# A third nested product in an attention output projection, with ScalarE reading the plain products and GpSimd adding them

## The chip, the cores and the metric

The kernel runs on one core of a Trainium2 chip. TensorE (PE) does the matrix products, VectorE (DVE), ScalarE (ACT) and GpSimd (POOL) work around it, SyncE (SP) issues most of the transfers, and each takes its instructions in a written order. Results of TensorE land in PSUM; operands and results of the others lie in SBUF. The metric is the device time of one execution in microseconds (us), lower being better; the median of three executions is quoted.

## The reference, cut to what matters

The input `x` is 8 images of 512 channels by 1024 positions, all in float32. Each image goes through self-attention with a residual, and then through a non-local block whose last step is a normalisation over the whole batch:

```python
q = conv1x1(x, Wq, bq); k = conv1x1(x, Wk, bk); v = conv1x1(x, Wv, bv)   # 8 heads of 64 channels
attn = softmax(einsum('bhdn,bhdm->bhnm', q, k) * scale)
out = einsum('bhnm,bhdm->bhdn', attn, v).reshape(B, C, H, W)
x = x + conv1x1(out, Wp, bp)                       # "p": the output projection
g, theta, phi = conv1x1 of x, each to 256 channels # "tp": theta and phi together
f = einsum('bcn,bdn->bcd', theta, phi) / n
z = conv1x1(einsum('bcd,bdn->bcn', f, g), W_w, W_b) + x
z_hat = (z - mean over batch and positions) * rsqrt(var + eps) * gamma + beta
```

The change is in `p`, a product of a 512 x 512 weight with a 512 x 1024 matrix for each image, which is added into `x`.

## The kernel before, in words

Images are worked on one after the other in the loop over `b` (L1063 to L1209). Within an iteration TensorE goes through the attention of image `b`, the projections q, v and k of image `b + 1`, then `p` of image `b`, then `tp`, `g` and the rest of the non-local block of image `b`. All these projections use Strassen's scheme in Winograd's form: a matrix product is split into 2 x 2 blocks and done with seven block products instead of eight, with sums and differences of blocks formed beforehand. `SEVEN` (L286) lists them: which weight block, which data block, which PSUM slot, and which quarters of the result the slot is read into. Products that share a slot accumulate in it, so the slot is read once after each of them and the later reads hold the running sum.

A block product can itself be done by seven smaller products: it is then called nested. One plain product of `p` is four matmuls of 128 x 512; a nested one is seven matmuls of 128 x 256. In the profile each float32 matmul appears as two records. `nested` (L305) issues the small matmuls one step at a time, and the list of counts in `INNER` (L302) says how many steps follow each plain matmul. For `p` of the images 1 to 6 the list `FIVE` (L297) has five plain products, and two products are nested, (1, "21", "11") and (2, "t4", "21"). The images 0 and 7 use seven plain ones.

`seven` (L333) takes the four PSUM slots in the order of the list `free`: the plain products use the first two, the nested ones the last two. Each slot holds 128 x 1024 numbers. After a product with nested partners, `free` is rotated by one, so that the first slot of the next product (`tp`) is the second plain slot of `p`. A slot that is taken by the next product waits until everything that reads it has ended.

`project` (L775) is `p`: VectorE reads each plain product out of PSUM and adds it to the quarters of `x` it belongs to, with the bias where the quarter is first touched (L782), else without (L477). The nested products are read in the same way, 128 x 256 at a time. The result then serves `tp` as data, together with four differences of quarters, `t1` to `t4` (`more_sums`, L262).

What `p` reads is prepared by GpSimd during k of the next image: the normalised attention output `o` (L729), the sums of the nested blocks (`inner_sums`, L279), four differences of quarters of `o` (L267), and then k's own four last additions (L402, at the end of `six`, L383), in this order.

Weights are kept in device memory in units of one to three blocks and loaded again for each image (`fetch`, L160). `UNITS` (L117) says which blocks form a unit; a unit with two blocks has room for the inner sums of both, and units are loaded through a ring of four buffers. Instructions recorded with `pe`, `dve` or `sp` (one function, L62) keep the program's order on their engine; each engine does its own in order, and a waiting instruction holds those behind it.

Of the kernel before, what the change touches and what calls it, by code (L numbers as in the profile page):

```python
# [8 lines left out]
F32 = mybir.dt.float32  # L9
# [7 lines left out]
P = 128  # L17
# [13 lines left out]
def unshifted(ctx: ExitStack, tc: tile.TileContext, a: dict, out: bass.AP):  # L31
# [79 lines left out]
    for b in range(1, B):  # L111
# [2 lines left out]
    loaded, ahead = [], {"unit": [], "first": []}  # L114

    PAIRS = ((1, 6), (3, 4), (5, 2))
    UNITS = {"WqT": PAIRS, "WkT": PAIRS, "WvT": PAIRS, "WpT": ((1, 2), (3, 4, 5), (6,)), "tp": ((1, 2), (3, 4, 5), (6,)),  # L117
             "WgT": (range(7),)}
    WIDTH = 14 * P

# [39 lines left out]
    def fetch(w, n, t=None, dma=None):  # L160
        dma, name = dma or nc.sync, w.name
        if t is None:
            t = wf0.tile([P, 2 * w.half], F32, tag="w0", name=f"w0_{name}") if n == "first" else \
                wr.tile([P, WIDTH], F32, tag="w", name=f"w_{name}_{n}")
        blocks = w.place(n, t)
        if name in kept:
            of = kept["plain" if w.last else name][n]
            sp(dma.dma_start(w.whole(n) if w.last else w.tiles[n], of))
            return
        if n == 0:  # L170
            corner[name] = block(f"a21_{name}")[:, :, :w.half]
# [36 lines left out]
    def inner_weights(w, i):  # L208

        a11, a12, a22, a21, s2, s3, s4 = w.inner(i)  # L210
        return [lambda to=to, l=l, r=r, op=op: dve(nc.vector.tensor_tensor(to, l, r, op))
                for to, l, r, op in ((s3, a11, a21, ALU.subtract), (a21, a21, a22, ALU.add), (s2, a21, a11, ALU.subtract),
                                     (s4, a12, s2, ALU.subtract))]

    def nest(w, i):
        for one in inner_weights(w, i):
            one()
# [64 lines left out]
    def quarters_of(t):  # L282
# [16 lines left out]

    INNER = {"p": (FIVE, ((1, "21", "11", False), (2, "t4", "21", True)), [0] * 4 + [1] * 14),  # L302
             "tp": (FIVE, ((2, "t4", "21", True), (1, "21", "11", False)), [0] * 24 + [1] * 14)}

    def nested(name, w, data, tags, first, add, goes_to, positions_out):  # L305
# [25 lines left out]
                yield  # L331

    def seven(name, w, data, positions_out, first, add, between=None, early=False,  # L333
              by_chunk=False, inner=None):

        nk, half = w.shape[2], w.shape[3]
        tags = list(free)
        free[:] = [tags[3], tags[1], tags[0], tags[2]] if early else [tags[3], tags[1], tags[2], tags[0]]  # L340
        slots, begun = {}, set()
        steps, counts = iter(()), iter(())
        if inner:
            free[:] = [tags[1], tags[2], tags[3], tags[0]]
            products, goes_to, counts = INNER[inner]
            counts = iter(counts)
            steps = nested(name, w, data, tags[2:], first, add, goes_to, positions_out)
        else:
            products = LATER if early == "later" else EARLY if early else SEVEN

        def read(reads, ps):
            for to, is_first in reads:
                (first if is_first else add)(to, ps)

        for n, (what, wi, di, s, reads) in enumerate(products):
            if s not in slots or early and what == "t4":
                slots[s] = bank(tags[s], f"{name}_{s}_{n}")
                begun -= {one for one in begun if one[0] == s}
            ps, d = slots[s], data[di]
            if positions_out:  # L360
                parts = [(ps.rearrange("p h (i f) -> p (h i) f", f=half)[:, i, :], i * half // 512,
                          lambda k, i=i: d[:, k, i * P:(i + 1) * P], lambda k: w[:, wi, k, :])
                         for i in range(512 // P)]
            else:
                parts = [(ps[:, m, :], m, lambda k, m=m: w[:, wi, k, m * P:(m + 1) * P], lambda k: d[:, k, :])
                         for m in range(half // P)]
            work = [(*part, k) for part in parts for k in range(nk)]
            if by_chunk and what in ("11", "s1t1"):
                work.sort(key=lambda one: one[4])
            for i, (to_ps, at, lhsT, rhs, k) in enumerate(work):  # L370
                pe(nc.tensor.matmul(to_ps, lhsT(k), rhs(k), start=(s, at) not in begun, stop=(k == nk - 1),  # L371
                                    skip_group_check=True))
                begun.add((s, at))
                for _ in range(next(counts, 0)):
                    next(steps)
            read(reads, ps)
            if between and n in between:
                between[n]()

    SIX = (((1, "21", "11"), (6, "22", "12")), ((3, "t1", "22"), (4, "t2", "T6")), ((5, "t3", "T7"), (2, "t4", "21")))  # L380
    ORDER = "0a 0b 1a 2a 2b 1b 5a 4a 5b 4b 3a 3b 6a 6b".split()

    def six(name, w, data, positions_out, at, begin, third, fills, by_scalar=False):  # L383

        fills = dict(fills)
        shape = [P, 4, 256] if positions_out else [P, 2, 512]
# [75 lines left out]
        assert not fills, fills  # L462
        if by_scalar:
            add("T7", "T6")
        add("22", "T7")
        add("21", "T7")

    def rows(q):
        return q[0] if isinstance(q[0], slice) else slice((int(q[0]) - 1) * CC // 2, int(q[0]) * CC // 2)
# [65 lines left out]
    def heads_of(b, what, w, bias, data, pin=lambda ins: None, steps=None, fills=None, **how):  # L535

        t = mats.tile([P, CC, N], F32, tag=what, name=f"{what}_{b}")

        if fills is not None:
            def begin(to, ps, i):  # L540
                nc.scalar.activation(to, ps, AF.Identity, bias=bias[:, i:i + 1])

            def third(to, ps, of, i):
                if what == "q":
                    nc.scalar.activation(to, ps, AF.Identity, bias=steps[:, i:i + 1])
                else:
                    dve(nc.vector.scalar_tensor_tensor(to, ps, steps[:, i:i + 1], of, ALU.add, ALU.add))

            six(f"p{what}_{b}", w, data, False, lambda q: t[:, rows(q), cols(q)], begin, third, fills,
                what == "q")  # L550
# [12 lines left out]
        return t  # L563
# [211 lines left out]
    def project(b, xt, w, between, data):  # L775
# [12 lines left out]

# [274 lines left out]
    for b in range(B):  # L1063
        last = b == B - 1
        nxt = {}
        if b == 1:
            nest(w_tp, 1)
            nest(w_tp, 2)
            keep("tp", w_tp, (0,))
            load_w()  # L1070
# [39 lines left out]
        if not last:  # L1110
# [20 lines left out]
            k = heads_of(b + 1, "k", weights("WkT"), bk, data, dve, steps=dk, fills={  # L1131
                (0, 13): [*o_sums, *(more if b else ())], (1, 13): () if b else more,
                (2, 0): () if b else [lambda: dve(nc.vector.tensor_tensor(bp, bp, got, ALU.add)),
                                      lambda: weight_sums(w_p, corner["WpT"], (6,), dve, nc.gpsimd)]})
# [302 lines left out]
```

## Time and profile before

| | |
|---|---|
| median of three executions | 2103.23 us (2102.15 to 2103.65) |
| the profiled execution's own time | 2103.74 us |
| its span, from the first to the last instruction | 2102.0 us |
| TensorE busy | 2078.5 us, 99% of the span |
| VectorE busy | 1442.3 us, 69% |
| ScalarE busy | 788.6 us, 38% |
| GpSimd busy | 734.0 us, 35% |
| mean clock granted to TensorE | 0.996 of full speed |
| DMA queue of SP | 31.8% of the 16 engines' span |

A row of the groups of instructions reads: line, engine, operation, output and inputs by the program's names, shapes and count, then the busy time, the mean duration of one in ns, and the idle time just before them with what ended it. A row of the timeline reads: start, length, engine, line, operation, operands, count of merged instructions, and in brackets an idle time and what ended it. All times are us from the span's start unless marked ns. Matmuls are pipelined, so the spacing of their starts says more than their durations.

### The profile page before, as it was taken

Reading aid. Unit: us, or ns where it says so; the run is one execution under the profiler, and the core shown is the slowest. Engines: PE = TensorE matmul, PEld = TensorE weight load, DVE = VectorE, ACT = ScalarE, POOL = GpSimd, SP = SyncE. Lnnn points to the kernel's source line nnn. Section 1 sums busy time; section 2 is a strip of 40 time slices with the busy share of each in tenths; the row PEclk is TensorE's granted clock in tenths of the full one; section 3 lists DMA queues with packets and bytes.
Section 4 is the critical chain, followed back from the end, with each engine's and each line's share of the span. In section 5 each row is a group of like instructions: output and inputs, shape, how many; then the busy total and the mean of one; then the engine's idle time right before and its main releaser. Section 6 shows DMA issues by size and latency. Waiting matters only on the chain.

```text
span 2102.0 us, 34269 instructions
## 1 busy us (share of the span) xinstructions
PE 2078.5 (99%) x13646; PEld 1170.3 (56%) x13646; DVE 1442.3 (69%) x2169; ACT 788.6 (38%) x1043; POOL 734.0 (35%) x637
## 2 busy tenths in 40 slices
PE   9999999999999999999999999999999999999995
PEld 4535864358733677336773377633776348743472
DVE  5587567875677656776567766677665775676756
ACT  1465203652046410464105641066312653056106
POOL 0024800348113581134812356123660338411010
PEclk9999999999999999999999999999999999999998
DMA  6254534345343443435324363253644345212668
GB/s 230 83 144 78 162 137 143 42 83 157 105 115 38 89 148 106 119 39 114 132 92 122 40 142 122 69 126 40 155 149 154 39 48 174 99 30 40 218 253 321
DMA packets 77263, 246.80 MB, mean 117 GB/s; under 512 B 17188, under 2 KB 25640, under 8 KB 75048
## 3 DMA queue, kind: packets, MB, share of 16 engines
q1 hardware_dynamic: 63224, 218.17, 31.8%
q0 software_dynamic: 12016, 24.80, 12.2%
q8 instruction: 110, 1.80, 0.4%
q10 hardware_dynamic: 1856, 1.56, 0.3%
q14 instruction: 57, 0.47, 0.1%
HBM read 163.20 MB, written 47.71 MB: 100 GB/s over the span
## 4 chain that ended last, share of the span: by engine, by line
PE 98%; ACT 1%; DVE 1%; DMA 0%; issue 0%; DVEq 0%
PE ps L611 21%; PE po L637 21%; PE pp L371 7%; PE ptp L371 7%; PE pv_in L447 6%; PE pq_in L450 6%; PE pk_in L450 6%; PE pg L371 5%; PE pz L371 3%; PE pf L866 2%; PE ptp_in_s L319 2%; PE pp_in_s L322 2%; PE pwf L909 1%; PE pv L414 1%; PE pq L417 1%; PE pq L371 1%
## 5 line engine op out<-in xcount | busy, mean ns | idle before, releaser
L614 ACT ACTIVATE e<-ps 128x1024 f32<-128x1024 f32 x512 | 522.4, 1024 | 428.7 <-PE ps L611 418.0
L667 POOL DMA_DIRECT2D fold<-acc x336 | 257.2, 816 | 949.2 <-DMA fold<-acc 450.4
L620 DVE TENSOR_TENSOR acc<-acc,e 128x1024 f32<-128x1024 f32 x384 | 469.9, 1224 | 94.5 <-ACT e L614 84.6
L611 PE MATMUL ps<-q,k 64*64 64x512 f32 x4096 | 529.3, 589 | 0.0
L637 PE MATMUL po<-e,v 64*64 64x512 f32 x4096 | 528.8, 589 | 0.0
L637 PEld LDWEIGHTS po<-e,v 64*64 64x64 f32 x4096 | 156.7, 133 | 282.8 <-issue 275.5
L611 PEld LDWEIGHTS ps<-q,k 64*64 64x64 f32 x4096 | 155.6, 133 | 283.1 <-issue 274.9
L897 ACT ACTIVATE g<-pg,gb 128x512 f32<-128x512 f32 x31 | 21.3, 687 | 447.7 <-PE pg L371 447.6
L618 DVE TENSOR_TENSOR acc<-e,e 128x1024 f32<-128x1024 f32 x64 | 78.3, 1224 | 117.6 <-ACT e L614 115.4
L371 PE MATMUL pp<-t_o,w_WpT 128*128 128x512 f32 x208 | 101.0, 592 | 0.0
L371 PE MATMUL ptp<-w_tp,t_x 128*128 128x256 f32 x400 | 96.1, 379 | 0.0
L729 POOL TENSOR_TENSOR o<-o,r 128x1024 f32<-128x1024 f32 x28 | 65.5, 2359 | 36.0 <-DMA r<-den_d 35.5
L371 PEld LDWEIGHTS ptp<-w_tp,t_x 128*128 128x128 f32 x400 | 72.3, 190 | 7.8
L458 DVE TENSOR_TENSOR k<-k,pk_in 128x256 f32<-128x256 f32 x112 | 46.8, 421 | 39.4 <-PE pk_in L450 35.0
L371 PE MATMUL ptp<-w_tp,x 128*128 128x256 f32 x272 | 69.6, 380 | 0.0
L371 PE MATMUL pp<-o,w_WpT 128*128 128x512 f32 x144 | 67.7, 592 | 0.0
L456 ACT COPY v<-pv_in 128x256 f32<-128x256 f32 x84 | 31.4, 374 | 95.8 <-DVE T_pv L458 25.5
L458 DVE TENSOR_TENSOR v<-v,pv_in 128x256 f32<-128x256 f32 x112 | 46.2, 421 | 29.3 <-PE pv_in L447 22.8
L456 ACT COPY k<-pk_in 128x256 f32<-128x256 f32 x84 | 31.2, 372 | 93.3 <-PE pk_in L450 91.6
L782 DVE SCALAR_TENSOR_TENSOR x<-pp,bp,x 128x512 f32<-128x512 f32 x52 | 37.5, 746 | 33.0 <-PE pp L371 33.0
L447 PE MATMUL pv_in<-w_WvT,i_t_x 128*128 128x128 f32 x448 | 59.2, 275 | 0.0
L450 PE MATMUL pk_in<-i_t_x,w_WkT 128*128 128x256 f32 x224 | 58.1, 381 | 0.1
(246 smaller groups left out, 3166.0 us busy)
## 6 DMA issues: line engine op xcount, KB each, us to landing
fold<-acc POOLq DMA_DIRECT2D x336, 64.0 KB, 3.0
w_WqT<-kept_WqT SPq DMA_DIRECT2D x21, 896.0 KB, 5.9
w_WvT<-kept_WvT SPq DMA_DIRECT2D x21, 896.0 KB, 5.5
w_WkT<-kept_WkT SPq DMA_DIRECT2D x21, 896.0 KB, 6.7
r<-den_d SPq DMA_DIRECT2D x32, 512.0 KB, 7.7
x<-in_x_dram SPq DMA_DIRECT2D x30, 512.0 KB, 6.0
spill<-x SPq DMA_DIRECT2D x24, 512.0 KB, 4.3
z<-spill SPq DMA_DIRECT2D x24, 512.0 KB, 8.1
```

What stands on the lines that cost most here:

```text
L371: pe(nc.tensor.matmul(to_ps, lhsT(k), rhs(k), start=(s, at) not in begun, stop=(k == nk - 1), skip_group_check=True))
L447: pe(nc.tensor.matmul(ps[:, i, :], d[:, i * P:(i + 1) * P], a, start=start and not i, stop=True, skip_group_check=True))
L450: pe(nc.tensor.matmul(ps, a, d, start=start, stop=True, skip_group_check=True))
L456: nc.scalar.copy(piece(q, i, j), ps)
L458: dve(nc.vector.tensor_tensor(piece(q, i, j), piece(q, i, j), ps, ALU.add))
L611: pe(nc.tensor.matmul(ps[c * P // 2:(c + 1) * P // 2, j, :], k[r, p, keys], q[r, p, h * 512:(h + 1) * 512], start=True, stop=True, skip_gr ...
L614: nc.scalar.activation(e, ps, AF.Exp, scale=SCALE)
L618: nc.vector.tensor_tensor(accs[u], es[u, 0], e, ALU.add)
L620: ins = nc.vector.tensor_tensor(accs[u], accs[u], e, ALU.add)
L637: pe(nc.tensor.matmul(ps[j * D:(j + 1) * D, r, :], v[keys, m, (2 * p + j) * D:(2 * p + j + 1) * D], e[keys, j, :], start=(m == 0), stop=(m ...
L667: nc.gpsimd.dma_start(to, of, accum_op=ALU.add)
L729: dve((engine or nc.vector).tensor_tensor(at, at, of, ALU.mult))
```

## The change

For the images 1 to 6, `p` gets a third nested product: `FIVE` gives way to `FOUR`, with four plain products, and the nested ones are now (6, "22", "12"), (2, "t4", "21") and (1, "21", "11"), in this order. The third nested product uses the same PSUM columns as the first. The last plain product, `s3t3`, takes a new tile in the second plain slot instead of accumulating in the first.

The plain products `s1t1` and `s2t2` are no longer read by VectorE. ScalarE copies each into a block in SBUF (two copies of 128 x 512), and GpSimd adds that block into the quarters it belongs to, two for `s1t1` and three for `s2t2` (128 x 1024 each). The last two additions of k on GpSimd are moved behind them (`later`). The difference `t1` of `tp`'s data moves ahead of the reads of the last plain product, and `t2` stands directly behind them.

Block 6 needs inner sums: for the units of WpT to have room, they become (1, 2), (3, 4), (5, 6). The inner sums of block 6 are made once, at the start of image 1, in a tile of their own (`nest_apart`), and stored; from then on block 5 and the widened block 6 are loaded with two transfers. For image 0 the sums of the weight blocks 5 and 6 go to VectorE, and the addition of the small bias goes from VectorE to GpSimd.

```diff
-    UNITS = {"WqT": PAIRS, "WkT": PAIRS, "WvT": PAIRS, "WpT": ((1, 2), (3, 4, 5), (6,)), "tp": ((1, 2), (3, 4, 5), (6,)),
+    UNITS = {"WqT": PAIRS, "WkT": PAIRS, "WvT": PAIRS, "WpT": ((1, 2), (3, 4), (5, 6)), "tp": ((1, 2), (3, 4, 5), (6,)),
...
-            sp(dma.dma_start(w.whole(n) if w.last else w.tiles[n], of))
+            if n == 2 and name == "WpT" and not w.last:
+                sp(dma.dma_start(w[5], of[:, 0, :].rearrange("p (k f) -> p k f", k=2)))
+                sp(dma.dma_start(w.tiles[n][:, WIDTH // 2:], kept["block 6"]))
+            else:
+                sp(dma.dma_start(w.whole(n) if len(of.shape) == 3 else w.tiles[n], of))
...
+    def nest_apart(w, n, i):
+
+        t = w3.tile([P, N], F32, tag="acc", name="apart")[:, :WIDTH // 2]
+        to = t[:, :2 * w.half]
+        sp(nc.sync.dma_start(to, kept["plain"][n][:, 1, :]))
+        w.at[i] = to.rearrange("p (k f) -> p k f", k=2)
+        w.extra[i] = t[:, 2 * w.half:].rearrange("p (i f) -> p i f", i=3)
+        nest(w, i)
+        kept[f"block {i}"] = dram.tile([P, WIDTH // 2], F32, tag=f"block{i}", name=f"block{i}")
+        sp(nc.sync.dma_start(kept[f"block {i}"], t))
...
-    INNER = {"p": (FIVE, ((1, "21", "11", False), (2, "t4", "21", True)), [0] * 4 + [1] * 14),
+    FOUR = (SEVEN[0], ("s1t1", 3, "t1", 1, (("22", False), ("12", False))),
+            ("s2t2", 4, "t2", 0, (("12", False), ("22", False), ("21", False))),
+            ("s3t3", 5, "t3", 1, (("22", True), ("21", False))))
+
+    INNER = {"p": (FOUR, ((6, "22", "12", True), (2, "t4", "21", True), (1, "21", "11", False)),
+                   [1] * 10 + [2, 1] + [2] * 4),
...
-            if s not in slots or early and what == "t4":
+            if s not in slots or early and what == "t4" or inner == "p" and what == "s3t3":
...
-            read(reads, ps)
+            if inner and ahead_of_last and n == len(products) - 1:
+                ahead_of_last()
+            if inner and what in via:
+                via[what](reads, ps)
+            else:
+                read(reads, ps)
...
-        add("22", "T7")
-        add("21", "T7")
+        ends = [lambda q=q: add(q, "T7") for q in ("22", "21")]
+        if later is not None:
+            later += ends
+            return
+        for one in ends:
+            one()
...
-                if b == B - 1 and q in ("11", "22"):
+                if b == B - 1 and q in ("11", "22") or b and ps.shape[-1] == 512 and q == "22":
                     dve(ins)
 
+        def by_scalar(reads, ps):
+            t = block(f"read_{b}")
+            for m in range(2):
+                nc.scalar.copy(t[:, m, :], ps[:, m, :])
+            for q, _ in reads:
+                at = xt[:, rows(q), cols(q)]
+                dve(nc.gpsimd.tensor_tensor(at, at, t, ALU.add))
+            if len(reads) == 3:
+                for one in later:
+                    one()
+
         seven(f"pp_{b}", w, data, False, first, add_to(xt), between, early=b == B - 1 and "later",
-              inner="p" if 0 < b < B - 1 else None)
+              inner="p" if 0 < b < B - 1 else None,
+              via={"s1t1": by_scalar, "s2t2": by_scalar}, ahead_of_last=lambda: more_sums(x1, (1,), dve))
...
         if b == 1:
+            nest_apart(Weights("WpT"), 2, 6)
             nest(w_tp, 1)
...
-                o_sums = [lambda: inner_sums(nxt["o"], "21", dve, nc.gpsimd), *o_sums]
+                o_sums = [*(lambda of=of: inner_sums(nxt["o"], of, dve, nc.gpsimd) for of in ("22", "21")), *o_sums]
...
-                more = [lambda i=i: weight_sums(w_p, corner["WpT"], (i,), dve, nc.gpsimd) for i in (3, 4, 5)]
+                more = [lambda i=i: weight_sums(w_p, corner["WpT"], (i,), dve, nc.gpsimd) for i in (3, 4)]
...
-                (2, 0): () if b else [lambda: dve(nc.vector.tensor_tensor(bp, bp, got, ALU.add)),
-                                      lambda: weight_sums(w_p, corner["WpT"], (6,), dve, nc.gpsimd)]})
+                (2, 0): () if b else [lambda: dve(nc.gpsimd.tensor_tensor(bp, bp, got, ALU.add))]})
+            if b == 0:
+                weight_sums(w_p, corner["WpT"], (5, 6), dve)
...
-        project(b, xt, w, between, nxt["o"])
+        x1 = data_sums(quarters_of(xt), f"x1_{b}", ())
+        project(b, xt, w, between, nxt["o"], x1, later if 0 < b < B - 1 else ())
...
-        data = data_sums(quarters_of(xt), f"x1_{b}", (1, 2, 3, 4) if last else (1, 2))
+        data = x1
+        if 0 < b < B - 1:
+            more_sums(data, (2,), dve)
+        else:
+            more_sums(data, (1, 2, 3, 4) if last else (1, 2))
```

More of the change, by code (lines that the diff above doesn't have):

```diff
@@ L333, in seven @@
     def seven(name, w, data, positions_out, first, add, between=None, early=False,
-              by_chunk=False, inner=None):
+              by_chunk=False, inner=None, via=(), ahead_of_last=None):
         nk, half = w.shape[2], w.shape[3]
@@ L381, in unshifted, with six @@
     ORDER = "0a 0b 1a 2a 2b 1b 5a 4a 5b 4b 3a 3b 6a 6b".split()
-    def six(name, w, data, positions_out, at, begin, third, fills, by_scalar=False):
+    def six(name, w, data, positions_out, at, begin, third, fills, by_scalar=False, later=None):
         fills = dict(fills)
@@ L549, in heads_of @@
             six(f"p{what}_{b}", w, data, False, lambda q: t[:, rows(q), cols(q)], begin, third, fills,
-                what == "q")
+                what == "q", how.get("later"))
             return t
@@ L773, in attention, with project @@
         return o["o"], all_denominators, normalize
-    def project(b, xt, w, between, data):
+    def project(b, xt, w, between, data, x1, later=()):
         def first(q, ps):
@@ L1126, in unshifted @@
                 more = [lambda: inner_sums(nxt["o"], "t4", dve, nc.gpsimd)]
-                o_sums = [lambda: inner_sums(nxt["o"], "21", dve, nc.gpsimd), *o_sums]
+                o_sums = [*(lambda of=of: inner_sums(nxt["o"], of, dve, nc.gpsimd) for of in ("22", "21")), *o_sums]
             else:
                 w_p = loaded[1]
-                more = [lambda i=i: weight_sums(w_p, corner["WpT"], (i,), dve, nc.gpsimd) for i in (3, 4, 5)]
-            k = heads_of(b + 1, "k", weights("WkT"), bk, data, dve, steps=dk, fills={
+                more = [lambda i=i: weight_sums(w_p, corner["WpT"], (i,), dve, nc.gpsimd) for i in (3, 4)]
+            later = [] if b else None
+            k = heads_of(b + 1, "k", weights("WkT"), bk, data, dve, steps=dk, later=later, fills={
                 (0, 13): [*o_sums, *(more if b else ())], (1, 13): () if b else more,
-                (2, 0): () if b else [lambda: dve(nc.vector.tensor_tensor(bp, bp, got, ALU.add)),
-                                      lambda: weight_sums(w_p, corner["WpT"], (6,), dve, nc.gpsimd)]})
+                (2, 0): () if b else [lambda: dve(nc.gpsimd.tensor_tensor(bp, bp, got, ALU.add))]})
+            if b == 0:
+                weight_sums(w_p, corner["WpT"], (5, 6), dve)
         else:
```

## The prediction

> **What bounds the kernel now.** I first read the page's busy shares and chain, then TensorE's waits.
>
> ```profile
> PE 2078.5 (99%) x13646; PEld 1170.3 (56%) x13646; DVE 1442.3 (69%) x2169; ACT 788.6 (38%) x1043; POOL 734.0 (35%) x637
> ...
> PE 98%; ACT 1%; DVE 1%; DMA 0%; issue 0%; DVEq 0%
> ```
>
> ```profile
> PE count L1223 <- DVE good L1221: 8.6, 1, 8.6
> PE warm_ps L500 <- DVE zeros L483: 1.1, 1, 1.1
> PE pk_in L450 <- DVE T_pk L547: 1.1, 1, 1.1
> ```
>
> TensorE is the path, and it waits three times in all. So matmul time removed is time saved, and any new wait of TensorE is lost one for one: nothing on the path can absorb it. Next I read the timeline around `p` of image 1, for TensorE and then GpSimd and VectorE.
>
> ```profile
> 514.38 3.60 PE L371 MATMUL pp<-o,w_WpT 128*128 128x512 f32 x8
> 517.82 1.02 PE L371 MATMUL pp<-t_o,w_WpT 128*128 128x512 f32 x2
> 518.67 0.59 PE L322 MATMUL pp_in_s<-o,w_WpT 128*128 128x256 f32 x2
> 519.11 1.02 PE L371 MATMUL pp<-t_o,w_WpT 128*128 128x512 f32 x2
> ...
> 537.59 3.62 PE L371 MATMUL ptp<-w_tp,x 128*128 128x256 f32 x16
> ```
>
> ```profile
> 502.28 0.73 POOL L279 TENSOR_TENSOR i_o<-o 128x256 f32<-128x256 f32 x1
> ...
> 517.51 2.36 POOL L402 TENSOR_TENSOR k<-k 128x1024 f32<-128x1024 f32 x1
> 519.95 6.96 POOL L402 TENSOR_TENSOR k<-k,T_pk 128x1024 f32<-128x1024 f32 x3
> 541.42 2.35 POOL L267 TENSOR_TENSOR t_x<-x,t_x 128x1024 f32<-128x1024 f32 x1 [14.51 <-DVE t_x L267]
> ```
>
> ```profile
> 533.07 1.22 DVE L477 TENSOR_TENSOR x<-x,pp 128x1024 f32<-128x1024 f32 x1 [0.44 <-PE pp L371]
> ...
> 537.79 2.35 DVE L477 TENSOR_TENSOR x<-x,pp 128x1024 f32<-128x1024 f32 x2 [1.23 <-PE pp L371]
> 540.06 1.22 DVE L267 TENSOR_TENSOR t_x<-x,t_x 128x1024 f32<-128x1024 f32 x1
> ```
>
> Four plain matmuls take 517.82 - 514.38 = 3.44 us, so 0.86 each; a plain and a nested one take 519.11 - 517.82 = 1.29, so a nested one takes 0.43. `p` lasts 537.59 - 514.38 = 23.21 us, which is 20 x 0.86 + 14 x 0.43: no gap. GpSimd is busy without a break until 526.9, well into `p`. VectorE's reads of the last plain product (537.79 to 540.1) run while TensorE is already in `tp`. That works because `tp`'s first slot is the second plain slot of `p`, whose last read (533.07) had ended at 534.29.
>
> **What the Trainium skill says.** "Perfetto Trace Analysis", under Tensor Engine Instruction, says that VectorE, ScalarE and GpSimd are strictly first in, first out; the trace's rows stand in program order, so a waiting read holds the later ones. "GPSIMD Engine Reference", section 3, has a two-input add about 1.96 times slower than on VectorE; here it is 2.35 against 1.22 us for 128 x 1024, 1.93 times. "SBUF — State Buffer", Who interferes with whom, says that a VectorE operation with two SBUF inputs contends with GpSimd's reads: the bias add of 128 x 4 on VectorE took 2.30 us (249.34 to 251.64) under a GpSimd operation that ended at 251.62. "TensorE: Matmul & The Clock Gate", Part 1, says that an idle window of about 3.4 us halves the clock, and that a busy one restores it. The windows at the end agree: the last product ends at 2080.5, and the granted clock then falls.
>
> ```profile
> 2075.00:2080.00 5.00, 5.00 (x13) 2.09 (x11) 4.21 (x7) 5.00 (x6) 0.00 (x0) 1.00 1.01 401
> 2080.00:2085.00 5.00, 0.52 (x2) 0.00 (x0) 4.51 (x11) 4.32 (x5) 0.00 (x0) 0.94 1.02 407
> 2085.00:2090.00 5.00, 0.19 (x2) 0.11 (x2) 4.04 (x8) 3.84 (x4) 0.00 (x0) 0.50 1.02 407
> ```
>
> A mean of 0.94 over 5 us is 0.6 us at half speed, so it fell at 2084.4, 3.9 us after the last product. At the start, the first matmul begins at 1.07 and the first 128 x 512 record still takes 4.64 to 5.50, twice 0.43: some 4.4 us at half speed.
>
> **Matmuls, image by image (times from the start S of p; S = 514.38 in image 1).** 16 x 0.86 + 21 x 0.43 = 22.8 us against 23.2: 0.4 us saved per image, 2.6 us for six. That is all the arithmetic gives.
>
> **GpSimd.** The inner sums of quarter 22 add four operations of 0.72 ahead of everything (2.9 us). The first two k additions then end at 522.3 + 2.9 = 525.2, S + 10.8. The other two move behind `p`'s additions, where nobody needs them before the next attention. The eighth plain matmul (`s1t1`) ends at S + 10.1. ScalarE, idle here since 515, copies 2 x 0.58 us (the 128 x 512 copy of L642 means 581 ns): ready at S + 11.3. GpSimd's two additions end at S + 16.0. The twelfth plain matmul (`s2t2`) ends at S + 15.7, its copies at S + 16.9, and its three additions follow at 2.32 to 2.4 us each: quarter 12 at S + 19.3, 22 at 21.6, 21 at 24.0.
>
> **The first new wait.** The seventh step of the second nested product is read into quarter 21 by VectorE. It runs on TensorE at about S + 16.8, but in program order its read stands behind GpSimd's third addition, which writes the same quarter. VectorE therefore waits from about S + 18.3 (after the read of the step that follows) to S + 24.1 and reads until S + 24.6. Behind it stand all the remaining reads. In the built program TensorE's second matmul of the third nested product waits for exactly this read, because they share a PSUM tile. TensorE reaches it at S + 18.5 and starts again at S + 24.7: 6.2 us idle.
>
> **The second new wait.** What is left is three times two nested and two plain matmuls, 6 x 0.43 + 2 x 0.86 = 4.3 us: `p`'s matmuls end at S + 29.0. `s3t3` lies in the second plain slot, the one that `tp` takes first, and VectorE's order after the last nested read is `t1`, two bias reads, one addition. In the built program `tp`'s first matmul waits for that last addition. Drain and last nested read 0.6, `t1` 1.2, two reads 1.4 (the pair in the timeline of L782), addition 1.2: S + 33.5. TensorE idles 4.5 us. Before, `tp` started at S + 23.2; now 10.3 us later, six times: +62 us, the saved 0.4 included. After that `tp` gains nothing and loses nothing: `t2` is ready 1.2 us after its start (3.7 before), `t4` and its inner sums as much earlier.
>
> **Clock.** Idle stretches of 6.2 and 4.5 us stand against the 3.9 us that one fall took. With a free-running window of 3.4 us (the skill) the first contains a whole one in (6.2 - 3.4) / 3.4 = 8 of 10 cases, the second in 3 of 10. Each fall costs half of some 4.4 us, 2.2 us. About 1.1 falls per image give 6 x 1.1 x 2.2 = 14 us; bounds are none, 0 us, and two each, 26 us.
>
> **The rest.** The bias add on GpSimd removes the wait of 1.1 us in image 0 (VectorE sat in that 2.30 us add). Taken at nothing: VectorE's two weight sums in image 0 (2 x 0.69 us; cover: 3.4 us of idle before the first read of `p`; uncovered they cost 1.4 us once). The separate preparation of block 6 in image 1 (four operations of 0.29 us and one load, which VectorE waits for among attention sums; it has some 0.8 us to spare in each step of 2.06 us, and twelve blocks ahead; bound 3 us once). The extra transfer: block 5 and the widened block 6 are issued where unit 2 was, at about 508.5, and land in 2.7 (256 KB) to 4.5 us (896 KB), so by 513.5, against a first need at 515.2, earlier than before (S + 10.3). Cover 1.7 us; uncovered, each us costs 6. Two more ring blocks per image are taken when k's ten are free.
>
> **Sum.** 62 - 1 + 14 = +75 us on the span of 2102.0, so 2177; the execution lies 1.7 us and the median 1.2 us above the span: about 2177.
>
> **Rivals.**
> - The clock holds, since the idle stretches are broken by 4.3 us of matmuls: 2103 + 61 = 2164. For it: the threshold rests on one fall. Chance 0.2.
> - Every idle stretch drops it: 2103 + 61 + 26 = 2190. For it: 6.2 and 4.5 us both exceed 3.9. Chance 0.15.
> - Only one of the two waits is real, as VectorE could have drained more of the tail than I give: 6.2 x 6 - 1 = 36 us and no clock loss at the end, some 2140 to 2150. Chance 0.07.
> - Not slower: GpSimd's addition into quarter 21 ends before VectorE gets to its read and `s3t3`'s reads hide in `tp`. Then only 2.6 + 1.1 us are gained: 2099.5, within 0.2%. This decides if the three additions take under 0.8 us instead of 7.1. Against it: all 128 x 1024 additions of GpSimd in the trace mean 2345 to 2359 ns. Chance 0.03. A gain above 0.2% (4.2 us) would need more than that whole saving.
> - The change does what it says about products; its claim of another slot holds too, and that slot is the trouble.
>
> **How the numbers follow.** The forecast, both waits and about one fall of the clock per image, has 0.55: 2177, its own range 2168 to 2186. The range 2158 to 2194 takes in the cases without and with all falls, and half a us of error per image on each wait (3 us); it leaves out the one-wait case and no change. The bound of 0.2%, 4.2 us, is about what a measurement of this kernel can tell from no change: slower 0.95, within it 0.03, faster 0.02.
>
> **What would show it.** TensorE's waits would list two new kinds with six entries each: `pp_in_s` on VectorE's bias read, about 6 us, and `ptp` on VectorE's L506 addition, about 4.5 us; VectorE would wait some 6 us for GpSimd. `p` would last 33 us from its start to `tp`'s. The clock would show below 0.99. Wrong would be: waits of `p`'s first nested matmul on a transfer; `tp` starting within a us of `p`'s end; a busy share still at 99%.

## The result, and the profile after

The changed kernel takes 2187.14 us (median of six executions, 2185.91 to 2188.01) against 2103.23 us before (here of six executions too, 2102.15 to 2103.65): a ratio of 1.040, 95% interval 1.0386 to 1.0413. It is 83.9 us slower. The profiled execution took 2186.95 us and its span is 2185.2 us.

The page of the changed kernel gives the busy time of each engine and, further down, the shares of the chain that ended last:

```profile
PE 2102.2 (96%) x13682; PEld 1190.1 (54%) x13682; DVE 1445.2 (66%) x2192; ACT 802.2 (37%) x1067; POOL 813.2 (37%) x690
...
PE 92%; POOL 3%; DVE 2%; ACT 1%; DMA 1%; issue 0%; SPq 0%; ACTq 0%; POOLq 0%; DVEq 0%
```

TensorE fell from 99% to 96% of the span, and for the first time GpSimd stands in the chain with 3%. Nor is the gap all idleness: TensorE's busy time rose by 23.7 us, although there is less matmul work. Its waits in the changed kernel (total, times, longest, in us), and then VectorE's only listed wait for GpSimd, which has the same count:

```profile
PE pp_in_s L342 <- DVE x L811: 34.5, 6, 5.8
PE ptp L391 <- DVE x L506: 25.3, 6, 4.2
...
PE pq L391 <- DMA w_WqT<-in_WqT_dram: 0.2, 1, 0.2
```

```profile
DVE x L811 <- POOL x L821: 33.7, 6, 5.6
```

There are two new waits, once per image each, 59.8 us together; the wait of 1.1 us in `k` of image 0 is gone. The last line says who kept VectorE: GpSimd's additions into `x`. The timeline of image 1, where `p` starts at 514.48 (514.38 before), shows both places:

```profile
531.38 6.94 POOL L821 TENSOR_TENSOR x<-x,read 128x1024 f32<-128x1024 f32 x3 [0.99 <-ACT read L818]
538.36 0.48 DVE L811 SCALAR_TENSOR_TENSOR x<-pp_in_s,bp,x 128x256 f32<-128x256 f32 x1 [5.62 <-POOL x L821]
538.89 2.08 PE L342 MATMUL pp_in_s<-i_o,w_WpT 128*128 128x256 f32 x4 [5.75 <-DVE x L811]
...
546.69 1.40 DVE L811 SCALAR_TENSOR_TENSOR x<-pp,bp,x 128x512 f32<-128x512 f32 x2
548.01 1.21 DVE L506 TENSOR_TENSOR x<-x,pp 128x1024 f32<-128x1024 f32 x1
549.27 5.23 PE L391 MATMUL ptp<-w_tp,x 128*128 128x256 f32 x16 [4.22 <-DVE x L506]
```

GpSimd's three additions end at 538.3; VectorE's bias read starts within 0.1 us, TensorE's nested matmul 0.5 us later. The second wait ends when the addition of 548.01 has read the last plain product out of the slot that `tp` takes first. Note the lengths too: four records of the nested matmul take 2.08 us, and `tp`'s first sixteen 5.23 us, where the kernel before needed 3.62. That is the clock. The view by windows shows it, here with windows of 3.41 us laid on the clock's own changes (columns: window, its length, then busy time of TensorE's matmuls, its weight loads, VectorE, ScalarE and GpSimd with counts, mean granted clock, DMA share, GB/s):

```profile
531.89:535.30 3.41, 1.25 (x4) 0.38 (x2) 0.42 (x1) 0.00 (x0) 3.41 (x2) 1.00 0.47 193
535.30:538.71 3.41, 0.00 (x0) 0.00 (x0) 0.35 (x1) 0.00 (x0) 3.41 (x3) 0.50 0.00 0
538.71:542.13 3.42, 3.24 (x6) 2.19 (x7) 0.97 (x3) 0.00 (x0) 3.42 (x2) 0.50 0.00 0
542.13:545.54 3.41, 2.92 (x11) 1.71 (x9) 1.69 (x4) 0.00 (x0) 0.80 (x1) 1.00 0.06 16
545.54:548.95 3.41, 0.00 (x0) 0.00 (x0) 3.41 (x4) 0.00 (x0) 0.00 (x0) 1.00 0.91 294
548.95:552.36 3.41, 3.09 (x7) 2.50 (x8) 1.40 (x2) 0.00 (x0) 1.86 (x1) 0.50 0.09 36
552.36:555.77 3.41, 3.41 (x17) 2.98 (x16) 1.23 (x1) 0.00 (x0) 3.25 (x5) 1.00 0.12 9
```

TensorE is at half speed in three windows per image, two after the first idle stretch began and one after the second. It matters only where matmuls run: 3.24 and 3.09 us here. Half of the busy time in all 18 such windows is 22.6 us.

By stage, from the first matmul of each stage to the first of the next: `p` of images 1 to 6 lasts 34.8 to 36.1 us (23.2 before), 72.6 us more in all; `tp` of these images 25.2 to 25.5 us (23.6 before), 10.2 us more in all. The other stages differ by at most 1.3 us, and these differences add up to 0.4 us. The 82.8 us of `p` and `tp` are 59.8 of waiting and 22.6 of half speed, less 2.4 of saved matmuls, with some 3 us of smaller stalls.

### The profile page after: what moved, and what is told of

The parts are those of the page before. It is cut to its first block, busy times and chain, and to the rows that moved or that the text cites. A ratio compares the mean times of both kernels' runs of the same rounds, so it can differ in the third digit from the quotient of the medians.

```text
span 2185.2 us, 34477 instructions
## 1 busy us (share of the span) xinstructions
PE 2102.2 (96%) x13682; PEld 1190.1 (54%) x13682; DVE 1445.2 (66%) x2192; ACT 802.2 (37%) x1067; POOL 813.2 (37%) x690
## 4 chain that ended last, share of the span: by engine, by line
PE 92%; POOL 3%; DVE 2%; ACT 1%; DMA 1%; issue 0%; SPq 0%; ACTq 0%; POOLq 0%; DVEq 0%
PE ps L640 20%; PE po L666 20%; PE ptp L391 7%; PE pq_in L475 6%; PE pp L391 5%; PE pv_in L472 5%; PE pk_in L475 5%; PE pg L391 4%; PE pz L391 3%; PE pp_in_s L342 2%; PE pf L907 2%; PE ptp_in_s L339 2%; POOL x L821 2%; PE pwf L950 1%; PE pv L439 1%; PE pq L442 1%
## 5 line engine op out<-in xcount | busy, mean ns | idle before, releaser
L391 PE MATMUL pp<-t_o,w_WpT 128*128 128x512 f32 x208 | 107.5, 619 | 0.3 <-DVE x L811 0.3
L391 PE MATMUL ptp<-w_tp,x 128*128 128x256 f32 x272 | 79.8, 424 | 25.3 <-DVE x L506 25.3
L758 POOL TENSOR_TENSOR o<-o,r 128x1024 f32<-128x1024 f32 x28 | 65.5, 2362 | 33.5 <-DMA r<-den_d 33.2
L391 PEld LDWEIGHTS ptp<-w_tp,t_x 128*128 128x128 f32 x400 | 72.3, 190 | 7.8
L821 POOL TENSOR_TENSOR x<-x,read 128x1024 f32<-128x1024 f32 x30 | 69.6, 2348 | 12.9 <-ACT read L818 12.9
L391 PEld LDWEIGHTS ptp<-w_tp,x 128*128 128x128 f32 x272 | 54.2, 216 | 35.6 <-DVE x L506 27.7
L811 DVE SCALAR_TENSOR_TENSOR x<-pp_in_s,bp,x 128x256 f32<-128x256 f32 x48 | 23.2, 484 | 70.5 <-PE pp_in_s L342 36.8
L342 PE MATMUL pp_in_s<-i_o,w_WpT 128*128 128x256 f32 x96 | 34.8, 463 | 34.5 <-DVE x L811 34.5
L506 DVE TENSOR_TENSOR x<-x,pp_in_s 128x256 f32<-128x256 f32 x78 | 32.8, 421 | 51.1 <-PE pp_in_s L342 50.9
L481 ACT COPY v<-pv_in 128x256 f32<-128x256 f32 x84 | 31.4, 374 | 95.8 <-DVE T_pv L483 25.5
L483 DVE TENSOR_TENSOR v<-v,pv_in 128x256 f32<-128x256 f32 x112 | 46.3, 422 | 29.3 <-PE pv_in L472 22.8
```

Of the source, the lines that this page charges most:

```text
L342: pe(nc.tensor.matmul(ps, a[wi], d[di], start=start, stop=True, skip_group_check=True))
L483: dve(nc.vector.tensor_tensor(piece(q, i, j), piece(q, i, j), ps, ALU.add))
L821: dve(nc.gpsimd.tensor_tensor(at, at, t, ALU.add))
```

## The experiments

My theory was: two independent waits, the first made by the order of GpSimd's additions, the second by the slot that `tp` is given, each with a price in clock on top; the third nested product itself costs nothing. The rivals: one wait that only shows in two places; waits without a clock price; or three nested products being too much reading for VectorE, whoever adds the rest.

### Another slot for `tp`

```diff
-            free[:] = [tags[1], tags[2], tags[3], tags[0]]
+            free[:] = ([tags[0], tags[2], tags[1], tags[3]] if inner == "p" else
+                       [tags[1], tags[2], tags[3], tags[0]])
```

> The changed kernel, with only the order in which p hands its PSUM slots to tp altered: tp's first slot is now the one that ScalarE read last, tp's second slot is one of the nested pair. No work is added or removed. My theory (two separate waits, each followed by a clock fall): the second idle stretch of TensorE goes from 4.2 us to under 1 us per image (quarter 11's last nested addition is left), the half-speed stretch of 3.4 us behind it goes with it (1.7 us), the first idle stretch stays at 5.7 us. 6 x (3.5 + 1.7) = 31 us less than the changed kernel: 2153 to 2160 us. Rival (tp waits for the sums of x that VectorE is late with, not for the slot): the idle stretch stays with another tile in its name, 2180 to 2187 us.

Measured: 2153.91 us (2152.14 to 2154.77), 33.2 below the changed kernel. TensorE's waits in this kernel:

```profile
PE pp_in_s L342 <- DVE x L812: 34.5, 6, 5.8
PE count L1273 <- DVE good L1271: 8.6, 1, 8.6
PE warm_ps L530 <- DVE zeros L513: 1.1, 1, 1.1
```

The wait of `tp` is gone whole, the other one is unchanged to a tenth, `tp` is back at 23.6 us. So it was the slot and not the sums of `x`, and the second wait is independent of the first.

### Another order of GpSimd's additions

```diff
-            ("s2t2", 4, "t2", 0, (("12", False), ("22", False), ("21", False))),
+            ("s2t2", 4, "t2", 0, (("21", False), ("12", False), ("22", False))),
...
-    INNER = {"p": (FOUR, ((6, "22", "12", True), (2, "t4", "21", True), (1, "21", "11", False)),
+    INNER = {"p": (FOUR, ((6, "22", "12", True), (1, "21", "11", False), (2, "t4", "21", True)),
```

> The changed kernel, with GpSimd's three additions after the third plain product in another order (quarter 21 first) and the last two nested products exchanged, so that quarter 21 gets its bias last. No work is added or removed. My theory (the first idle stretch is VectorE's bias read into quarter 21 behind GpSimd's third addition): the 5.75 us stretch goes to under 0.5 us, and the slow stretch behind it with it (1.8 us): 6 x 7.3 = 44 us less than the changed kernel, 2138 to 2148 us; the second idle stretch stays near 4 us, since VectorE's bias reads of quarter 22 now stand behind GpSimd's third addition. Rival (GpSimd is simply too late, the order only moves the wait): the stretch ahead of tp grows by what the first one gives up, 2175 to 2187 us.

Measured: 2155.21 us (2154.41 to 2156.02), 31.9 below the changed kernel, and 7 us above the range that I expected. Its waits:

```profile
PE ptp L391 <- DVE x L506: 34.7, 6, 5.8
PE count L1272 <- DVE good L1270: 8.6, 1, 8.6
PE pp_in_s L342 <- DVE x L811: 4.0, 6, 0.7
```

The first stretch went from 5.75 to 0.7 us. But the second grew from 4.2 to 5.8 us, which I had put at 4, and its half-speed stretch from one window to two. The next kernel's timeline shows where those 1.6 us come from.

### Both together

The two diffs above in one kernel.

> The changed kernel with both edits: slots handed to tp in another order, and GpSimd's additions and the last two nested products in another order. My theory: both idle stretches are under 1 us, TensorE's granted clock no longer falls in p and tp, p is 22.8 to 24 us long: 2187 - 83 = 2104, less up to 2 us: 2100 to 2110 us, within 0.2 per cent of the kernel before. Rival (one wait hides behind the other and a third one comes up, on quarter 22 or on the sum for the second product of tp): 2115 to 2145 us.

Measured: 2114.83 us (2114.75 to 2115.06), a ratio of 1.0054 to the kernel before, interval 1.0038 to 1.0071. That is 72.3 us below the changed kernel, just between the two expected ranges (up to 2110, from 2115): 11 us are left. The clock never falls (0.996 over the span). `p` is 23.73 us long (+0.5) and `tp` 25.0 (+1.4). First the additions to `k` and the first sum for `tp` in the changed kernel, then the end of `p` in this one:

```profile
538.27 4.66 POOL L427 TENSOR_TENSOR k<-k,T_pk 128x1024 f32<-128x1024 f32 x2
...
545.54 1.22 DVE L282 TENSOR_TENSOR t_x<-x 128x1024 f32<-128x1024 f32 x1
```

```profile
537.69 5.66 POOL L428 TENSOR_TENSOR k<-k,T_pk 128x1024 f32<-128x1024 f32 x2
538.27 2.86 DVE L282 TENSOR_TENSOR t_x<-x 128x1024 f32<-128x1024 f32 x1
541.06 1.40 DVE L812 SCALAR_TENSOR_TENSOR x<-pp,bp,x 128x512 f32<-128x512 f32 x2
...
545.91 3.72 PE L392 MATMUL ptp<-w_tp,t_x 128*128 128x256 f32 x16 [0.98 <-DVE tp L859]
```

VectorE's sum for `tp` takes 2.86 us beside GpSimd's two additions to `k`, and the pair 5.66 us, where it took 4.66 in the changed kernel and had ended before that sum began. All that follows on VectorE is 1.6 us late, up to the read of `tp`'s first slot, for which TensorE waits 0.98 us. These are k's last two additions, which the change moved to the end of `p`; I had costed that move at nothing.

### The additions to k out of the way

On top of the last kernel:

```diff
-            if len(reads) == 3:
-                for one in later:
-                    one()
...
         tp = theta_phi(b, w, data, tpb, between)
+        if 0 < b < B - 1:
+            for one in later:
+                one()
```

> The kernel with slots and additions in another order (2114.8 us), and beside that GpSimd's two last additions to k taken out of p's end and put behind GpSimd's sums for tp. If the 1.4 us per image that tp still loses come from these two additions (VectorE's first sum for tp took 2.86 us beside them and 1.22 us in the kernel before, and everything behind it on VectorE is late, at last the read of tp's first slot): tp is back at 23.6 us, 8.5 us less, 2104 to 2108 us; p's 0.5 us stay. If they come from the bias reads of quarter 22 behind GpSimd's third addition: 2112 to 2116 us.

Measured: 2106.64 us (2105.80 to 2107.33), 8.2 us less. In the same place of this kernel's timeline:

```profile
538.03 1.22 DVE L282 TENSOR_TENSOR t_x<-x 128x1024 f32<-128x1024 f32 x1
```

The sum is back at 1.22 us, `tp` at 23.6, `p` still at 23.73. So the 1.4 us per image were these two additions. The kernel with only the order of GpSimd's additions changed has the same sum at 2.85 us, which accounts for the 1.6 us there.

### The third nested product one plain matmul later

On top of that:

```diff
-                   [1] * 10 + [2, 1] + [2] * 4),
+                   [1] * 10 + [2, 1] + [1, 2, 2, 3]),
```

> The last kernel (slots, additions, and k's two additions moved; 2106.6 us) with one more edit: the third nested product starts one plain matmul later, its steps spread over p's last four plain matmuls as 1, 2, 2, 3 instead of 2, 2, 2, 2. If what p still loses against its 22.8 us of matmuls is TensorE's 0.67 us wait for VectorE's bias read behind GpSimd's first addition to quarter 21: that wait is gone, p is 23.1 us long, 6 x 0.6 = 3.6 us less, 2102 to 2104.5 us. If the wait only moves to p's last steps, where three nested steps now follow each other: no change, 2106 to 2108 us.

Measured: 2103.52 us (2103.05 to 2104.35), 3.1 us less, and a ratio of 1.0002 to the kernel before, 0.9993 to 1.0010. The 0.67 us wait for the first addition into quarter 21 is gone; this is the one wait of TensorE in `p` that is left, 0.17 us per image:

```profile
PE pp_in_s L342 <- DVE x L507: 1.0, 6, 0.2
```

`p` lasts 23.3 us, as long as before, so the 0.4 us of matmuls saved per image still go in this wait and in smaller stalls. With this all of the 83.9 us are traced: four edits, none of which adds or removes an operation, bring the changed kernel back to the kernel before.

### The clock alone

Both waits stay, and matmuls whose result nobody reads fill TensorE's idle time:

```diff
                 for _ in range(next(counts, 0)):
+                    if inner == "p":
+                        done.append(1)
+                        if len(done) == 16:
+                            fill(6)
                     next(steps)
+                if inner == "p" and len(done) == 21 and n == len(products) - 1 and i == len(work) - 1:
+                    fill(4)
```

Here `fill(n)` multiplies block 0 of the weights with quarter 11 of `o` into `p`'s first slot n times.

> The changed kernel with both waits left as they are, and TensorE's two idle stretches per image filled with matmuls whose result nobody reads: six of 128x512 ahead of the nested matmul that waits (about 5.2 of the 5.75 us), four ahead of tp's first (about 3.4 of the 4.2 us). If the clock falls are a cost of their own (10.8 us in p and 10.3 us in tp over six images), they go: 2187 - 21 = 2166 us (2160 to 2170), granted clock of the span back near 0.99, p near 33 us and tp near 23.6. If the waits alone make the loss, or the extra matmuls push the waiting ones back: 2183 to 2195 us.

Measured: 2169.07 us (2168.26 to 2170.20), 18.1 us less than the changed kernel, with 60 more matmuls. Its timeline at the first stretch:

```profile
532.97 5.31 PE L376 MATMUL pp_fill<-o,w_WpT 128*128 128x512 f32 x12
538.90 1.13 PE L342 MATMUL pp_in_s<-i_o,w_WpT 128*128 128x256 f32 x4 [0.62 <-DVE x L825]
```

The nested matmul starts at 538.90 as it did without the filling (538.89), and its four records take 1.13 us, not 2.08. So the waits are as long as they were, and the half speed was a cost of its own; the clock of the span is 0.996. The gain is 3 us short of the 21 that I expected. The rest lies in `tp`, still 5.5 us longer over the six images than before: it now reaches some of its weights before they have landed, and its waits for a transfer add up to 3.5 us.

```profile
PE ptp L399 <- DMA w_tp<-kept_tp: 3.5, 6, 1.3
```

### Three nested products read by VectorE

This asks whether the product needs GpSimd at all. The plain products come in another order, so that two of the seven additions happen in PSUM (the other edits are told in the expectation):

```diff
-    FOUR = (SEVEN[0], ("s1t1", 3, "t1", 1, (("22", False), ("12", False))),
-            ("s2t2", 4, "t2", 0, (("12", False), ("22", False), ("21", False))),
-            ("s3t3", 5, "t3", 1, (("22", True), ("21", False))))
+    FOUR = (SEVEN[0], ("s2t2", 4, "t2", 0, (("12", True),)),
+            ("s1t1", 3, "t1", 1, (("22", True), ("12", False))),
+            ("s3t3", 5, "t3", 0, (("22", False), ("21", False))))
...
-              via={"s1t1": by_scalar, "s2t2": by_scalar}, ahead_of_last=lambda: more_sums(x1, (1,), dve))
+              ahead_of_last=lambda: more_sums(x1, (1,), dve))
```

> The third nested product without ScalarE's and GpSimd's part: the plain products in the order 11, s2t2, s1t1, s3t3, with s3t3 again on top of 11 and s2t2 in p's first slot, so that VectorE has five reads of plain products (12 with bias; 22 with bias, 12; 22, 21) where the changed kernel has seven quarters to add to; nested products in the order 6, 1, 2; k's last two additions where the kernel before has them. My theory (the third nested product itself costs nothing and saves 0.4 us of TensorE per image; all of the loss is in who reads the plain products, in which order and from which slot): VectorE has some 18 us of reads in p's 22.8 us, no idle stretch of TensorE over 0.7 us in p and tp, 2103.5 - 2.4 - 1.1 = 2100 us (2097 to 2105). Rival (three nested products leave VectorE too many reads, and TensorE waits for them whoever adds the rest): p and tp longer by 1 to 3 us per image, 2108 to 2122 us.

Measured: 2116.80 us (2116.45 to 2118.26), ratio 1.0065 (1.0051 to 1.0079): the rival's range, but only in part for its reason. `p` is 25.5 us long. In image 1:

```profile
520.80 0.74 DVE L811 SCALAR_TENSOR_TENSOR x<-pp,bp,x 128x512 f32<-128x512 f32 x1
521.64 1.10 PE L391 MATMUL pp<-t_o,w_WpT 128*128 128x512 f32 x2 [1.45 <-POOL i_t_o L294]
...
533.01 1.40 DVE L811 SCALAR_TENSOR_TENSOR x<-pp,bp,x 128x512 f32<-128x512 f32 x2
534.33 1.21 DVE L506 TENSOR_TENSOR x<-x,pp 128x1024 f32<-128x1024 f32 x1
536.02 1.10 PE L342 MATMUL pp_in_s<-i_t_o,w_WpT 128*128 128x256 f32 x4 [0.80 <-DVE x L506]
```

The larger wait, 1.45 us, is a fault of my order. `s2t2` goes on top of 11 in the same slot directly after it, so its first matmul has to wait until VectorE has read 11 out (520.80 + 0.74 = 521.54; the matmul starts at 521.64). The profile puts it down to a GpSimd sum that had ended before; in the built program the matmul waits for that read. The smaller one, 0.80 us, is the rival's: a nested read that stands behind 2.6 us of reads of a plain product. As both waits are in one run, the run does not decide whether VectorE alone could read three nested products without a loss in a better order.

### Three nested products with one addition by GpSimd

So the order stays as in the changed kernel, ScalarE reads only `s2t2`, and four nested steps stand between `s2t2` and `s3t3`, which again shares its slot:

```diff
+    FOUR = (SEVEN[0], ("s1t1", 3, "t1", 1, (("22", True), ("12", True))),
+            ("s2t2", 4, "t2", 0, (("12", False),)),
+            ("s3t3", 5, "t3", 0, (("22", False), ("21", False))))
...
+    INNER = {"p": (FOUR, ((6, "22", "12", False), (1, "21", "11", False), (2, "t4", "21", True)),
+                   [1] * 10 + [0, 4, 2, 1, 2, 2]),
...
+              via={"s2t2": by_scalar}, ahead_of_last=lambda: more_sums(x1, (1,), dve))
```

> Three nested products, but of the plain ones only s2t2 is read by ScalarE, and GpSimd has one addition (quarter 12): order 11, s1t1, s2t2, s3t3 as in the changed kernel, s1t1 read by VectorE (22 and 12 with bias), s3t3 again on top of 11 and s2t2 in p's first slot (22, 21), four nested steps between s2t2's last matmul and s3t3's first, so that ScalarE's 1.1 us copy is over by then; nested order 6, 1, 2; k's additions and the slots for tp as in the kernel before. My theory: nothing on VectorE stands behind GpSimd but the first sum for tp, tp's first slot was read 10 us earlier; p 22.8 to 23.1 us, tp 23.6: 2103.1 - 1.3 - (0.6 to 2.4) = 2099.4 to 2101.2 us, the first version below the kernel before. Rival (five reads of plain products and 21 nested ones are too many for VectorE in p, as in the version without GpSimd, where TensorE waited 0.8 us for a nested read): p 23.5 to 24.5, 2103 to 2110 us.

Measured: 2102.34 us (2101.75 to 2103.92), a ratio of 0.9997 to the kernel before, 0.9988 to 1.0005: not to be told from it. The profile lists no wait of TensorE in `p` or `tp`, and `p` lasts 23.15 us. Of the 0.4 us that the arithmetic saves per image, 0.06 arrive. The four nested steps that now stand in a row, from 528.01 on, take the rest:

```profile
528.01 0.59 PE L342 MATMUL pp_in_s<-o,w_WpT 128*128 128x256 f32 x2
528.44 0.59 PE L342 MATMUL pp_in_s<-i_o,w_WpT 128*128 128x256 f32 x2
529.12 0.70 PE L342 MATMUL pp_in_s<-o,w_WpT 128*128 128x256 f32 x2
529.65 0.60 PE L342 MATMUL pp_in_s<-i_o,w_WpT 128*128 128x256 f32 x2
...
528.64 0.85 DVE L506 TENSOR_TENSOR x<-x,pp_in_s 128x256 f32<-128x256 f32 x2 [1.01 <-PE pp_in_s L342]
```

The third and the fourth step start 0.68 and 0.53 us after the one before them, instead of 0.43. In the built program the third waits for VectorE's read of the first, whose PSUM slot it writes, and the fourth for the read of the second; these are the two reads in the last row, which begin at 528.64 and end at 529.49. So three nested products can be had without a measurable loss. What is left to gain, at most 6 x 0.35 = 2.1 us, is about what these measurements can tell from nothing (the interval is 3.6 us wide).

### The bias sum alone

The kernel before, with one word changed:

```diff
-                (2, 0): () if b else [lambda: dve(nc.vector.tensor_tensor(bp, bp, got, ALU.add)),
+                (2, 0): () if b else [lambda: dve(nc.gpsimd.tensor_tensor(bp, bp, got, ALU.add)),
```

> The kernel before with one edit: the sum of p's bias (128x4) in image 0 is GpSimd's instead of VectorE's. If the 1.3 us that k of image 0 lost in the changed kernel are this edit's: TensorE's one wait of 1.1 us in k of image 0 is gone, k of image 0 is 21.8 us long instead of 23.1, and the time is 1 to 1.4 us below the kernel before, 2102.3 us or so, which is about what rounds of this size can tell. If they come from the weight sums that left GpSimd's and VectorE's queues there: no change, and the wait is still there.

Measured: 2102.68 us (2102.32 to 2103.79), ratio 0.9998 (0.9989 to 1.0006). `k` of image 0 is indeed 1.3 us shorter, and its wait is gone. But `p` of image 0 is 1.1 us longer, and its timeline shows why:

```profile
260.35 2.07 DVE L782 SCALAR_TENSOR_TENSOR x<-pp,bp,x 128x512 f32<-128x512 f32 x3 [6.07 <-POOL bp L1133]
261.90 0.67 PE L371 MATMUL pp<-t_o,w_WpT 128*128 128x512 f32 x1 [0.85 <-DVE x L782]
```

GpSimd comes to the sum late, VectorE's first read of `p` waits for it, and TensorE for that read. The edit gives up a wait of 1.1 us in `k` and makes `p` of image 0 1.1 us longer, 0.85 of it this wait. I had expected the first half only.

## Why the prediction was right, and where not

**Matmuls.** In the version with one addition by GpSimd `p` came to 23.15 us, of which 0.35 are the stalls shown there; 22.8 us of matmuls stands.

**First wait.** Right in place, owner and size: 5.75 us against 6.2, VectorE's bias read behind GpSimd's third addition. GpSimd's three additions end at S + 23.8 (forecast 24.0). Another order of the same work takes it to 0.7 us.

**Second wait.** Right in place and cause: 4.22 us against 4.5. Another slot takes it to nothing. The rival with only one real wait (2140 to 2150) is out; removing either leaves the other.

**Clock: the term that was mis-sized.** I took a fall to need a whole idle window of 3.4 us, which gave 1.1 falls per image and 14 us. There were two falls per image, in all six images, 22.6 us by the records and 18.1 us by the filling (21.6 with the transfers' 3.5 us that came up there). With 22.6 in place of 14 the forecast would have been about 2186, against 2187.1 measured. The rival "every idle stretch drops it" had this right and still ended at 2190, since its waits were 0.7 us per image too long and its falls 0.6 us per image too dear. "The clock holds" (2164) would have looked like the filled kernel, 2169.

**Costed at nothing, and wrong.** k's two last additions at `p`'s end: cover was there for their result, but not for VectorE's sum beside them. That cost nothing visible in the changed kernel, where they ran from 538.27 to 542.93 and the sum began at 545.54, after the first wait had put it off; it costs 8.2 us once that wait is gone (shown with the other slot in place). The Trainium skill's page "SBUF — State Buffer", section Who interferes with whom, which I had applied to the bias sum alone, speaks of this case; 2.86 against 1.22 us agrees with it. The two weight sums on VectorE in image 0, put at 0.69 us each, took 2.73 and 2.83 us beside GpSimd's work. The bias sum's gain of 1.3 us in `k` of image 0 is there, but in this execution `p` of image 0 is 0.55 us longer and `q` of image 0 is 0.69. These two vary: with the same code for image 0, the kernel with another slot for `tp` had a `p` of image 0 as long as before and a `q` 0.15 us shorter, and the version read by VectorE alone a `p` 1.25 us longer. What decides between them was not tested.

**Costed at nothing, and right.** The preparation of block 6, the extra transfer and the two ring blocks: no stage of images 0 and 1 except `p` and `tp` of image 1 is longer by more than 0.7 us, and TensorE's waits name no transfer in `p`.

**Sum.** 2177 against 2187.1, inside the range. On the span, +75 against +83.2: the clock 8.6 us more than forecast, the waits 4.4 less, small stalls of half a microsecond per image, which I had not counted, 2.8 more, and all other stages, from which I had expected 1 us less, 1.4 more (8.4 in all, of which 0.2 are rounding). The remaining 1.9 us are those by which the median lies above the span; my sum named 1.2 of them and then left them out. The number is inside the range with two terms off, of which one made up for a part of the other: falls too few, waits too long. That part is luck. The chances that I gave for slower add up to 0.97, not to the 0.95 of my last line.

## What to carry to other kernels

On a path that is 99% one engine, look at who has to read a result out before that engine may go on, and in which order the reader gets there; here the order and the slots of the same operations decided over 84 us, with the clock that follows the waits, and the matmuls saved over 2. When work is handed to a slower engine, ask which quarter the fast engine needs first and have that one done first, and ask which slot the next stage takes first and give it the one read longest ago. After removing a wait, look at the timeline again: the engine that no longer waits now runs beside work that it did not meet before.

## What the runs showed of the hardware that I had not expected

**When the clock falls.** The granted clock changes only at points 3.413 us apart, whose phase differs from run to run, and a window need not be idle as a whole. Of the 24 idle stretches of 4.2 to 5.8 us in `p` and `tp` of three kernels (the changed one, the one with another slot, the one with another order of additions), each one dropped the clock. At full speed, every window with up to 1.40 us of matmuls (41%) was followed by half speed, and none with 1.43 us (42%) or more; this holds in the traces of all eleven kernels of this document. The two windows nearest the border are in the kernel with the other slot, and in the one with the other order of additions:

```profile
530.31:533.73 3.42, 1.43 (x5) 0.55 (x3) 0.42 (x1) 0.00 (x0) 3.42 (x2) 1.00 0.53 210
533.73:537.14 3.41, 0.00 (x0) 0.00 (x0) 0.19 (x1) 0.00 (x0) 3.41 (x3) 1.00 0.00 0
```

```profile
1853.94:1857.36 3.42, 1.40 (x6) 0.70 (x4) 2.54 (x4) 0.00 (x0) 3.42 (x2) 1.00 0.43 116
1857.36:1860.77 3.41, 0.00 (x0) 0.00 (x0) 3.41 (x4) 0.00 (x0) 3.41 (x2) 0.50 0.63 229
```

The clock column of the second line (1.00 in the first view, 0.50 in the second) is the answer to the busy time of TensorE in the line above it. Window ends are known to some 0.05 us, so the border is "near 1.4 us". At half speed, windows 90% busy or more brought full speed back, and windows 70% busy or less did not. From the border follows an estimate for a TensorE that is busy otherwise: an idle stretch over twice 59% of a window, 4.0 us, drops the clock wherever it lies, one under 2.0 us never, and between them the phase decides. The Trainium skill's page "TensorE: Matmul & The Clock Gate", Part 1, has the window's 3413 ns and that it is free-running, and both agree; its "idle window" is one with less than some 41% of work in it here. The six stretches of 1.45 us in the version read by VectorE alone left the clock at full speed, as it says; none between 1.45 and 4.2 us occurred, so the estimate is untested there.

**What two engines cost each other.** A 128x1024 sum on VectorE with two SBUF inputs took 2.86 us beside GpSimd's additions and 1.22 us without; GpSimd's pair, which the sum ran beside, took 5.66 instead of 4.66 us.
